# Three vectors of a two-layer graph and state-space kernel reach all partitions by DMA through DRAM instead of by TensorE, with a new table of steps

## Chip, cores and metric

The kernel runs on one core of a Trainium2 chip. The metric is the device time of one execution in microseconds (us).

## What is computed

x has shape (32, 512, 256): 32 elements of 512 tokens with 256 features; adj has shape (32, 512, 512) and holds 0 and 1. All is fp32. Each element passes two layers, each of a graph part and a feed-forward part, with a layer norm ahead of each and a residual sum after it:

```python
x = x + gat(layernorm(x), adj)      # softmax over j of leaky_relu(f1_i + f2_j) where adj, times Wh
x = x + mamba2(layernorm(x))        # projection, convolution over 4 tokens, scan with 8 heads, output
x = x + gru(gat(layernorm(x), adj), layernorm(x))
x = x + moe(layernorm(x))           # shared MLP + 4 experts, the two best by softmax of x @ gW
```

Three pieces matter here.

- **Attention.** The softmax's exponential of a leaky ReLU is written as a maximum of two products, exp(f1)exp(f2) and exp(0.2 f1)exp(0.2 f2), suitably shifted. So a query factor per token i and a key factor per token j are enough. The matrix is made with j on partitions and i along the row, so the query factors, two rows of 512, have to be present on all 128 partitions.
- **Scan.** The tokens of an element are cut into four pieces of 128. Each state that a piece inherits is weighted by exp of the running sum of dA up to each token, per head. These decays are needed as a row of 128 tokens on all 64 partitions of a head's state.
- **Mixture.** The output of expert e for token i is multiplied by a gate g(i, e). Hidden rows of two experts lie on 64 partitions each with tokens along the row, so g has to be present on 64 partitions.

## The kernel before

TensorE (PE in the profile) does the products, VectorE (DVE), ScalarE (ACT) and GpSimd (POOL) what stands between; SyncE (SP) issues the loads and stores. The weights are loaded once, ahead of the loop, by DMAs issued from ACT.

**Buffers.** `quad` tiles (16 buffers of some 4 KB a partition) hold x, xT, xn, L, query and the like; `row` tiles (26 of 2 KB) hold rows of 512; `bank` is one of the eight PSUM banks, each 128 x 512. A tile's buffer is used again once its last reader is done.

**The order is written out by hand.** An element's work is cut into 20 parts (`PARTS`), each a generator that yields after each small step. `PLAN` gives a turn to each step of each part, `PERIOD` is the distance between successive elements in turns, and all steps of all elements are sorted by `b * PERIOD + turn`. The engines' instruction streams have that order, and each engine runs its own in order, waiting where an input or a buffer isn't ready. A turn has no fixed length; a period of turns has one element's worth of steps, from four or five neighbouring elements.

**The steps concerned.**

- `attention` (L271): the largest f2 by a reduction (L276), a transpose that puts it on all partitions (L279), its maximum (L282) and three multiples (L285). Four transposes of f1, broadcast over 128 columns, put f1 on all partitions (L290, bank `ps_f1`). ACT makes the two query factors from this by ReLU (L294) and exp (L297), each 128 x 512, and the key factors from f2 (L300, L302). For each of four j, ACT multiplies by key1 (L309), DVE takes the maximum with the second product (L312) and masks by adj (L315). The result pT is read by PE at L343 in layer 0 and at L675 in layer 1.
- `steps_of_time` (L382): dt, dA and its running sums by TensorE (L428), laid out with piece and head on partitions as `byS` and `byL`. `byHL` (L436) spreads byL over heads; from both, TensorE makes the differences (L445, two groups with four banks each) and ACT their exponentials (L451, L454), the L of the scan. Then 12 products with a matrix of ones at chosen rows (`kind1`, L461) spread the running sums over 64 partitions in three banks, and ACT takes their exponentials into `ecs` rows (L468).
- `scan` (L546) reads ecs at L577 (last column, for the state) and L579 (POOL multiplies it with C); TensorE uses the product at L620.
- `gates` (L757): few gate logits per token by `narrow`, softmax, the two best, new weights g5 with four repeats (L807) and a column of ones (L798), four transposes (L812), copied as `gT` (L815).
- `mixture` (L860): two products of gT with `pair_of` (L868) spread the gates over partitions, four products with `b3` (L873) start the output with the biases; DVE multiplies the experts' hidden rows by the gates (L877); TensorE adds the shared part and the experts (L884, L886) in two banks, DVE adds them to x (L888), and x is stored (L891).

SP's stream per element has ten DMAs: x (L259), two times four of adj (L267), and the output (L891). None of them feeds on what the kernel itself computed except the last.

Of the kernel before, what the change touches and what calls it, by code (L numbers as in the profile page):

```python
# [11 lines left out]
F32 = mybir.dt.float32  # L12
# [6 lines left out]
P = 128  # L19
N = 512  # L20
# [11 lines left out]
def adj_ffn_kernel(ctx: ExitStack, tc: tile.TileContext, i: dict, out: bass.AP):  # L32
# [36 lines left out]
    pair_of = const.tile([HD, P], F32, name="pair_of")  # L69
    for j in range(2):  # L70
        nc.vector.tensor_copy(pair_of[32 * j:32 * j + 32].rearrange("e (s g) -> e s g", s=2),
                              ident[32 * j:32 * j + 32, 34 * j:34 * j + 2].unsqueeze(2).to_broadcast([32, 2, HD]))
# [8 lines left out]
    kind1 = const.tile([P, HD], F32, name="kind1")  # L81
    nc.vector.tensor_copy(kind1, kinds[:, 1:].to_broadcast([P, HD]))
# [115 lines left out]
    for r in (64, 96):  # L198
        nc.scalar.dma_start(b3[r:r + 4, :], i["L1_ffn_eb3"])
        nc.scalar.dma_start(b3[r + 4:r + 5, :], i["L1_ffn_sb3"].unsqueeze(0))  # L200
# [14 lines left out]
    small = ctx.enter_context(tc.tile_pool(name="small", bufs=2))  # L215

# [54 lines left out]
    def attention(f1, f2, adj, kind):  # L271
# [16 lines left out]
        pf = bank("ps_f1")  # L288
        for t in range(T):
            nc.tensor.transpose(pf[:, t * P:(t + 1) * P], f1[:, t:t + 1].to_broadcast([P, P]), ident)  # L290
        yield
        query = quad("query", 2)
        for n, scale in enumerate((-0.8, 0.8)):
            nc.scalar.activation(query[:, n, :], pf, AF.Relu, scale=scale, bias=nfs[:, n + 1:n + 2])  # L294
            yield
        for n in range(2):
            nc.scalar.activation(query[:, n, :], query[:, n, :], AF.Exp, scale=-1.0)  # L297
            yield
# [7 lines left out]
        for j in range(0, T, 2):  # L306
# [7 lines left out]
            for i, p in both:  # L314
                nc.vector.scalar_tensor_tensor(p, adj[i].bitcast(kind), 2.0 ** -120, p, op0=ALU.max, op1=ALU.min)  # L315
                yield
# [13 lines left out]
    def gnn0(e):  # L330
# [6 lines left out]
        pT = yield from attention(f21[:, 1, :], f21[:, 0, :], e.adj, U32)  # L337
# [28 lines left out]
    def narrow(name, w, vT):  # L366
# [8 lines left out]
        few = small.tile([P, P], F32, name="fewT")  # L375
# [6 lines left out]
    def steps_of_time(e):  # L382
# [51 lines left out]
        yield  # L434
        byHL = quad("byHL", HEADS)
# [5 lines left out]
        e.ecss = [None]  # L441
        for h0 in (0, 4):
# [5 lines left out]
            for c in range(0, T, 2):  # L448
# [4 lines left out]
                for L, _ in both:  # L453
                    nc.scalar.activation(L, L, AF.Exp, scale=-1.0)  # L454
                    yield

        banks = [bank("ps_ecs") for c in range(1, T)]
        for q in range(2):
            for c, ps in enumerate(banks, 1):
                for r in range(2):  # L460
                    nc.tensor.matmul(ps[r * HD:(r + 1) * HD, q * 2 * P:(q + 1) * 2 * P], kind1[32 * c:32 * c + 32, :],  # L461
                                     byHL[32 * c:32 * c + 32, heads_of(q, r), :], start=q == 0, stop=True,
                                     skip_group_check=True)
        yield
        for ps in banks:
            ecs = row("ecs")
            e.ecss.append(ecs.rearrange("p (j l) -> p j l", j=NP))
            nc.scalar.activation(ecs, ps, AF.Exp)  # L468
            yield
# [193 lines left out]
    def gnn1(e):  # L663
# [5 lines left out]
        pT = yield from attention(f21[:, 1, :], f21[:, 0, :], e.adj, I32)  # L669
# [87 lines left out]
    def gates(e):  # L757
# [38 lines left out]
        g5 = row("g5").rearrange("p (t r e) -> p t r e", t=T, r=4)  # L796
        nc.gpsimd.memset(g5[:, :, :, 5:], 0.0)
        nc.gpsimd.memset(g5[:, :, :, 4:5], 1.0)  # L798
# [7 lines left out]
        for t in range(T):  # L806
            nc.vector.tensor_mul(g5[:, t, :, :4], lg[:, t, :].unsqueeze(1).to_broadcast([P, 4, 4]),  # L807
                                 red[:, t:t + 1].unsqueeze(2).to_broadcast([P, 4, 4]))
        yield
        ps = bank("ps_gT")  # L810
        for t in range(T):
            nc.tensor.transpose(ps[:, t * P:(t + 1) * P], g5[:, t, :, :].rearrange("p r e -> p (r e)"), ident)  # L812
# [182 lines left out]
```

## Time and profile before

| | |
|---|---|
| time, median of 3 runs | 3431.26 us (3430.89 to 3432.96) |
| the profiled execution's own time | 3430.99 us |
| its span in the profile | 3429.3 us |
| busy PE / DVE / ACT / POOL | 3367.4 / 2814.7 / 1694.0 / 587.8 us |
| mean granted TensorE clock | 0.996 of full |
| DMA | 110.45 MB, mean 32 GB/s |

In the views of the profile, a line has the kernel's line (L290), the engine, the operation and the tiles `out<-in` with buffer numbers left out; "x256" is a number of instructions. A group shows the busy time and the mean of one in ns, then the idle time of the engine just before it and what ended it. An fp32 product shows as two matmul records (x4 for two products); a transpose as one. Some groups of this profile, as count, mean ns of one and busy us:

| line, what | count | mean ns | busy us |
|---|---|---|---|
| L290 PE, f1 onto partitions | 256 | 275 | 38.9 |
| L461 PE, decays onto partitions | 768 | 387 | 35.4 |
| L868 PE, gates onto partitions | 128 | 640 | 36.1 |
| L873 PE, biases | 256 | 400 | 36.2 |
| L812 PE, gates transposed | 128 | 272 | 19.2 |
| L294 / L297 ACT, query factors | 128 / 128 | 684 / 627 | 81.0 / 73.3 |
| L468 ACT, decays | 96 | 597 | 50.4 |
| L312 / L315 DVE, pT | 256 / 256 | 859 / 681 | 212.0 / 166.5 |
| L807 / L888 DVE | 128 / 64 | 166 / 680 | 13.5 / 43.5 |
| L392 ACT, 128 x 32 | 32 | 229 | 7.3 |

Matmuls are pipelined: the printed lengths overlap, and busy time is their union.

### The profile page before, as it was taken

How to read it: one execution, taken by the hardware profiler on the slowest of the kernel's cores; microseconds unless marked ns; L12 is line 12 of the kernel's file. 1: busy time of each engine (PE TensorE's matmuls, PEld its weight loads, DVE VectorE, ACT ScalarE, POOL GpSimd, SP SyncE). 2: the span in 40 equal slices, each digit the busy share in tenths (PEclk: the TensorE clock that was granted, in tenths of full speed). 3: DMA queues.
4: the chain of work that ended last, by engine and by line, in shares of the span. 5: the costliest groups of instructions: out<-in, count | busy, mean ns of one | idle time of the engine just before them, and what ended most of it. 6: DMA issues, size and time to landing. Idle time of an engine off the chain costs nothing.

```text
span 3429.3 us, 49262 instructions
## 1 busy us (share of the span) xinstructions
PE 3367.4 (98%) x17800; PEld 1979.2 (58%) x17800; DVE 2814.7 (82%) x7625; ACT 1694.0 (49%) x3202; POOL 587.8 (17%) x593
## 2 busy tenths in 40 slices
PE   5999999999999999999999999999999999999998
PEld 3555655565555656555655556565556555565654
DVE  6888888888888888888888888888888888888873
ACT  2455455444555454554445554445544455544453
POOL 0112111112111121111121111221111211112210
PEclk8999999999999999999999999999999999999999
DMA  3001011011001010110110110101101100101000
GB/s 127 22 28 38 22 38 28 25 38 38 23 28 34 29 38 22 37 28 25 38 38 22 28 34 29 38 22 38 28 26 38 38 22 28 35 28 38 19 19 13
DMA packets 78392, 110.45 MB, mean 32 GB/s; under 512 B 8122, under 2 KB 44100, under 8 KB 78148
## 3 DMA queue, kind: packets, MB, share of 16 engines
q1 hardware_dynamic: 71216, 101.34, 9.9%
q10 hardware_dynamic: 6932, 5.96, 0.5%
q8 instruction: 141, 2.31, 0.3%
q14 instruction: 103, 0.84, 0.1%
HBM read 90.50 MB, written 16.78 MB: 31 GB/s over the span
## 4 chain that ended last, share of the span: by engine, by line
PE 95%; DVE 2%; issue 1%; ACT 0%; POOL 0%; DMA 0%; SPq 0%; DVEq 0%; POOLq 0%; ACTq 0%
PE ps_conv L476 8%; PE ps_g L675 7%; PE ps_rz L701 6%; PE ps_mo L657 6%; PE ps_e L837 6%; PE ps_z L538 6%; PE ps_h L343 6%; PE ps_rz L704 6%; PE ps_y L612 3%; PE ps_s L828 3%; PE ps_e L886 3%; PE ps_hn L714 3%; PE ps_g L351 3%; PE ps_in L726 3%; PE ps_seg L445 3%; PE ps_xT L252 2%
## 5 line engine op out<-in xcount | busy, mean ns | idle before, releaser
L483 DVE SCALAR_TENSOR_TENSOR acc<-ps_conv,cw,acc 128x511 f32<-128x511 f32 (+2 forms) x480 | 345.3, 736 | 51.0 <-ACT acc L480 46.5
L734 POOL TENSOR_TENSOR oT<-xT,gate 128x512 f32<-128x512 f32 x64 | 121.0, 1912 | 1130.0 <-ACT gate L731 1130.0
L476 PE MATMUL ps_conv<-xT,win 128*128 128x512 f32 x640 | 291.4, 594 | 0.2 <-ACT xT L254 0.2
L224 POOL TENSOR_TENSOR rstd<-rstd,mhalf 128x4 f32<-128x4 f32 x128 | 160.7, 1256 | 737.9 <-DVE dtd L556 380.4
L254 ACT COPY xT<-ps_xT 128x512 f32<-128x512 f32 x192 | 106.1, 587 | 300.5 <-PE ps_xT L252 300.5
L675 PE MATMUL ps_g<-xn,pT 128*128 128x257 f32 x1024 | 246.9, 383 | 0.7 <-DVE pT L315 0.7
L675 PEld LDWEIGHTS ps_g<-xn,pT 128*128 128x128 f32 x1024 | 191.6, 190 | 92.9 <-issue 37.5
L701 PE MATMUL ps_rz<-xT,whh 128*128 128x512 f32 x512 | 244.0, 599 | 1.2
L538 PE MATMUL ps_z<-xT,win 128*128 128x512 f32 x512 | 242.0, 595 | 0.0
L704 PE MATMUL ps_rz<-go,wih 128*128 128x512 f32 x512 | 240.7, 592 | 0.0
L343 PE MATMUL ps_h<-pT,xn 128*128 128x512 f32 x512 | 231.8, 596 | 8.8 <-issue 8.8
L837 PE MATMUL ps_e<-xT,ew 128*128 128x512 f32 x512 | 236.6, 595 | 0.0
L579 POOL TENSOR_TENSOR ecs<-ecs,cc 128x512 f32<-128x512 f32 x96 | 136.1, 1418 | 546.3 <-DVE end L577 538.0
L657 PE MATMUL ps_mo<-wc,xh 128*128 128x256 f32 x1024 | 226.3, 379 | 0.0
L312 DVE SCALAR_TENSOR_TENSOR pT<-query,key,pT 128x512 f32<-128x512 f32 x256 | 212.0, 859 | 9.9 <-ACT pT L309 9.9
L657 PEld LDWEIGHTS ps_mo<-wc,xh 128*128 128x128 f32 x1024 | 192.1, 190 | 24.8
L476 PEld LDWEIGHTS ps_conv<-xT,win 128*128 128x128 f32 x640 | 121.7, 190 | 140.3 <-issue 137.1
L234 DVE BATCH_NORM_STATS2 st<-x 128x6 f32<-128x256 f32 x512 | 196.6, 416 | 3.3
L480 ACT ACTIVATE acc<-ps_conv,cb,cw 128x512 f32<-128x512 f32 x160 | 124.8, 780 | 138.0 <-PE ps_conv L476 137.4
L241 DVE TENSOR_SCALAR xn<-x,mv,rstd 128x256 f32<-128x256 f32 (+1 forms) x512 | 183.3, 410 | 5.4 <-POOL rstd L224 5.4
L325 DVE SCALAR_TENSOR_TENSOR prod<-xn,wrow 128x256 f32<-128x256 f32 x512 | 187.6, 417 | 0.0
L682 ACT ACTIVATE pT<-ps_g,rs 128x256 f32<-128x256 f32 x128 | 60.7, 474 | 236.8 <-DVE rs L679 236.8
(209 smaller groups left out, 7040.3 us busy)
## 6 DMA issues: line engine op xcount, KB each, us to landing
adj<-in_adjT_dram SPq DMA_DIRECT2D x256, 256.0 KB, 2.8
x<-in_x_dram SPq DMA_DIRECT2D x32, 512.0 KB, 3.9
out_dram<-x SPq DMA_DIRECT2D x32, 512.0 KB, 5.3
win<-in_L_ffn_W_in_dram ACTq DMA_DIRECT2D x1, 1160.0 KB
raw<-in_wihT_dram ACTq DMA_DIRECT2D x1, 768.0 KB, 7.4
whh<-in_whhT_dram ACTq DMA_DIRECT2D x1, 768.0 KB, 8.1
ew<-in_L_ffn_eW_dram ACTq DMA_DIRECT2D x5, 128.0 KB, 3.1
woutT<-in_woutT_dram ACTq DMA_DIRECT2D x1, 512.0 KB, 7.5
```

Source lines behind the costliest of these rows:

```text
L234: nc.vector.bn_stats(st[:, t, :], x[:, t, :])
L312: nc.vector.scalar_tensor_tensor(p, query[:, 1, :], key2[:, i:i + 1], p, op0=ALU.mult, op1=ALU.max)
L325: nc.vector.scalar_tensor_tensor(prod, xn[:, t, :D], 1.0, wrow[:, u, :], op0=ALU.mult, op1=ALU.mult, accum_out=f21[:, u, t:t + 1])
L343: nc.tensor.matmul(ps, xn[:, j, k * P:(k + 1) * P], pT[:, j, :], start=j == 0, stop=j == T - 1)
L476: nc.tensor.matmul(ps, win[:, k, 512 + c * P:512 + (c + 1) * P], e.xT[:, k, :], start=k == 0, stop=k == KD - 1)
L483: nc.vector.scalar_tensor_tensor(acc[:, s:], ps[:, :N - s], cw[:, c, 3 - s:4 - s], acc[:, s:], op0=ALU.mult, op1=ALU.add)
L538: nc.tensor.matmul(ps, win[:, k, j * P:(j + 1) * P], uT[:, k, :], start=k == 0, stop=k == KD - 1)
L657: nc.tensor.matmul(ps[:, :D], xh[:, j, t * P:(t + 1) * P], wc[:, j, :], start=j == 0, stop=j == NP - 1)
L675: nc.tensor.matmul(ps[:, :D + 1], pT[:, j, cut], xn[:, j, :], start=j == 0, stop=j == T - 1)
L701: nc.tensor.matmul(ps, whh[:, k, cols], xT[:, k, :], start=k == 0, stop=False)
L704: nc.tensor.matmul(ps, wih[:, k, cols], e.go[:, k, :], start=False, stop=k == KD - 1)
L837: nc.tensor.matmul(ps, ew1[:, k, m, :], vT[:, k, :], start=k == 0, stop=k == KD - 1)
```

## The change

- **Query factors.** The four transposes of f1 go. ACT makes the two factors by tokens, from the 128 x 4 tile f1, as q8 (128 x 2 x 4). A DMA stores q8 into a DRAM tile `line` of two rows of 512, and a second DMA loads `line` onto all 128 partitions as query.
- **Decays.** ACT takes the exponential of byL (128 x 128), a DMA stores it as `rows`, and a new part `decays_of_states` loads the three ecs rows with four DMAs each, every source row going to 64 partitions. The 12 products, their banks and the three exponentials go.
- **Gates.** g5 has no repeats: one product on DVE, one transpose, a copy of 128 x 128. A DMA stores it as `gates`, four DMAs load it as two `pg` rows, onto 64 partitions each. The products with pair_of go. The biases are made by four products in four row groups into four banks, and x is added per 128 tokens (four DVE additions of 256 columns instead of two of 512). b3 holds four copies of the biases, so the preamble has four more small DMAs on ACT.
- **DMAs.** All new ones in the loop are issued by SP, in the table's order: 32 per element.
- **Table.** 21 parts, PERIOD 424, and a new turn for every step of all parts.

```diff
-        pf = bank("ps_f1")
-        for t in range(T):
-            nc.tensor.transpose(pf[:, t * P:(t + 1) * P], f1[:, t:t + 1].to_broadcast([P, P]), ident)
+        q8 = small.tile([P, 2, T], F32, name="q8")
+        for n, scale in enumerate((-0.8, 0.8)):
+            nc.scalar.activation(q8[:, n, :], f1, AF.Relu, scale=scale, bias=nfs[:, n + 1:n + 2])
+        yield
+        nc.scalar.activation(q8, q8, AF.Exp, scale=-1.0)
+        yield
+        line = dram.tile([2, N], F32, name="line")
+        nc.sync.dma_start(line.rearrange("n (t p) -> p n t", p=P), q8)
         yield
         query = quad("query", 2)
-        for n, scale in enumerate((-0.8, 0.8)):
-            nc.scalar.activation(query[:, n, :], pf, AF.Relu, scale=scale, bias=nfs[:, n + 1:n + 2])
-            yield
-        for n in range(2):
-            nc.scalar.activation(query[:, n, :], query[:, n, :], AF.Exp, scale=-1.0)
-            yield
+        nc.sync.dma_start(query, line.partition_broadcast(P))
+        yield
...
+        eE = small.tile([P, P], F32, name="fewT", bufs=4)
+        nc.scalar.activation(eE, byL, AF.Exp)
+        yield
+        e.rows = dram.tile([P, P], F32, name="rows")
+        nc.sync.dma_start(e.rows, eE)
+        yield
...
+    def decays_of_states(e):
+
+        e.ecss = [None]
+        for c in range(1, T):
+            ecs = row("ecs").rearrange("p (j l) -> p j l", j=NP)
+            e.ecss.append(ecs)
+            for q in range(2):
                 for r in range(2):
-                    nc.tensor.matmul(ps[r * HD:(r + 1) * HD, q * 2 * P:(q + 1) * 2 * P], kind1[32 * c:32 * c + 32, :],
-                                     byHL[32 * c:32 * c + 32, heads_of(q, r), :], start=q == 0, stop=True,
-                                     skip_group_check=True)
...
+                    h = heads_of(q, r)
+                    src = e.rows[32 * c + HEADS + h.start:32 * c + HEADS + h.stop:2, :]
+                    nc.sync.dma_start(ecs[r * HD:(r + 1) * HD, 2 * q:2 * q + 2, :], src.partition_broadcast(HD))
             yield
...
+        nc.vector.tensor_mul(g5[:, :, :4], lg, red.unsqueeze(2).to_broadcast(shape))
         yield
         ps = bank("ps_gT")
-        for t in range(T):
-            nc.tensor.transpose(ps[:, t * P:(t + 1) * P], g5[:, t, :, :].rearrange("p r e -> p (r e)"), ident)
-        yield
-        gT = e.gT = row("gT")
-        nc.scalar.copy(gT, ps)
-        yield
+        nc.tensor.transpose(ps[:, :P], g5.rearrange("p t e -> p (t e)"), ident)
+        yield
+        gT = e.gT = small.tile([P, P], F32, name="fewT", bufs=4)
+        nc.scalar.copy(gT, ps[:, :P])
+        yield
+
+        line = dram.tile([P, P], F32, name="gates")
+        nc.sync.dma_start(line, gT)
+        yield
+        e.pgs = []
+        for j in range(2):
+            pg = row("pg")
+            e.pgs.append(pg)
+            for s in range(2):
+                src = line.rearrange("(t e) p -> e t p", t=T)[2 * j + s]
+                nc.sync.dma_start(pg[s * HD:(s + 1) * HD, :].rearrange("g (t p) -> g t p", t=T),
+                                  src.partition_broadcast(HD))
+            yield
...
+        pes = [bank("ps_e3") for t in range(T)]
+        for t, ps in enumerate(pes):
+            own = slice(32 * t, 32 * t + 32)
+            nc.tensor.matmul(ps[:, :D], gT[own, :], b3[own, :], start=True, stop=False)
+        yield
+        for t, ps in enumerate(pes):
+            tok = slice(t * P, (t + 1) * P)
+            nc.tensor.matmul(ps[:, :D], e.h2[:, tok], sw3, start=False, stop=False)
+            for j in range(2):
+                nc.tensor.matmul(ps[:, :D], e.e2[j][:, tok], ew3[:, j, :], start=False, stop=j == 1)
+            yield
+            nc.vector.tensor_add(x[:, t, :], ps[:, :D], x[:, t, :])
             yield
...
-    PERIOD = 420
+    PERIOD = 424
```

In the new table, the turns of the steps that matter, in an element's own count: layer 0's attention stores line at 138 and loads query at 213, ACT first reads it at 215, PE uses pT from 261 on. The exponential of byL is at 643, rows is stored at 644, ecs loaded at 690 to 692, first read (L577) at 727. Layer 1's attention has the transpose of the maximum at 882, q8 at 885 and 886, line at 887, query at 888, the keys at 889, L309 at 927 and 928, pT complete at 940, L675 from 958 on. The gates are stored at 1498 and loaded at 1549 and 1609; the mixture runs from 1634 to 1662, and the output is stored at 1850.

## The prediction

> **What bounds the kernel now.** I first read the page's shares and its chain of waits.
>
> ```profile
> PE 3367.4 (98%) x17800; PEld 1979.2 (58%) x17800; DVE 2814.7 (82%) x7625; ACT 1694.0 (49%) x3202; POOL 587.8 (17%) x593
> PE 95%; DVE 2%; issue 1%; ACT 0%; POOL 0%; DMA 0%; SPq 0%; DVEq 0%; POOLq 0%; ACTq 0%
> ```
>
> TensorE (PE) is 98% busy and is 95% of the chain that ends last; no DMA and no other engine is on it. A busy PE need not be at its peak, so I went on to the windows: stretches between the starts of the output matmuls (L657) of two successive elements, the stretch ahead of the first of these, and that after the last. The columns are length, then PE, PEld, DVE, ACT, POOL, clock, DMA share, GB/s.
>
> ```profile
> 1048.11:1152.74 104.63, 104.46 (x556) 61.51 (x556) 87.63 (x237) 52.88 (x100) 18.37 (x18) 1.00 0.11 31
> 2094.53:2199.16 104.63, 104.46 (x557) 61.52 (x556) 87.62 (x237) 52.88 (x100) 18.37 (x18) 1.00 0.10 31
> 0.00:118.52 118.52, 75.82 (x390) 42.86 (x391) 80.64 (x228) 38.52 (x73) 13.98 (x31) 0.90 0.33 105
> 3340.59:3429.30 88.71, 79.39 (x304) 45.26 (x302) 35.30 (x116) 27.04 (x50) 6.47 (x9) 0.97 0.04 13
> ```
>
> In the middle an element costs 104.63 us of PE. DVE needs 87.6, ACT 52.9, and the DMA engines are 11% used: all three have room. Only the head has long PE gaps. So time is bought by taking columns off PE, provided nothing new makes it wait. What a step takes on PE I read as the distance from its start to the next start in the PE timeline, since the printed durations overlap:
>
> ```profile
> 1720.49 0.60 PE L290 MATMUL ps_f<-ident,f 128*128 128x128 f32 x4
> 1720.92 1.88 PE L704 MATMUL ps_rz<-go,wih 128*128 128x512 f32 x4
> ...
> 1728.89 0.70 PE L868 MATMUL ps_gb<-gT,pair_of 32*128 32x512 f32 x2
> ...
> 1730.07 1.98 PE L701 MATMUL ps_rz<-xT,whh 128*128 128x512 f32 x4
> ...
> 1737.46 2.12 PE L445 MATMUL ps_seg<-byHL,byS 32*128 32x512 f32 x8
> 1739.51 0.70 PE L884 MATMUL ps_e<-sw,h 128*128 128x256 f32 x2
> ...
> 1743.92 1.14 PE L445 MATMUL ps_seg<-byHL,byS 32*128 32x512 f32 x8
> 1744.99 0.66 PE L563 MATMUL ps_xt<-ident,xh 128*128 128x128 f32 x4
> ...
> 1752.90 1.11 PE L461 MATMUL ps_ecs<-byHL,kind 32*64 32x256 f32 x24
> 1753.94 0.66 PE L586 MATMUL ps_st<-xdd,bt 128*64 128x128 f32 x8
> ```
>
> A transpose takes 0.43 / 4 = 0.108 us. A pair of 512-column matmuls (x4) takes 1.72. Two L445 groups of the same shape take 2.05 and 1.07: the first holds about 0.98 us of waiting for banks that the busy figure hides. The x24 of L461 take only 1.04, because six of them run side by side.
>
> **What the Trainium skill says.** "TensorEngine Tiling (Array Packing)", Key Properties: changing the tile shape drains TensorE. The trace agrees: the matmuls of L701 that follow the 32-row ones take 1.82 us (1730.07 to 1731.89) where 1.72 is usual, so 0.1 us a change. "TensorE: Matmul & The Clock Gate", Part 1: after an idle window the array runs at a lower clock; here the head's clock is 0.90. "DMA: Bandwidth & Descriptors", Specifications: below 512 bytes a write is a read-modify-write; no packet of the trace of before stores to DRAM so small, so no run here shows its price.
>
> **The change part by part, per element, on PE.**
> - Query factors: two attentions lose four transposes each (L290): 8 x 0.108 = 0.87 us.
> - Decays: L461 goes: 1.04 us.
> - Gates: four transposes (L812) become one: 3 x 0.108 = 0.33.
> - Bias and gates (L868, L873): 1.18 us, of which 2 x 0.43 is streaming of 512 columns and 0.32 loading and changing shape. What stays is four 256-column products in four row groups, side by side: 2 x 0.216 + 0.32 = 0.75. Saved 0.43 (0.25 if the passes do not overlap, 0.75 if the overhead halves).
>
> Sum: 2.67 us. **The new table** also moves every other step. Along both tables I count 26 changes of tile shape in a period before and 22 after, of which about two are in the prices above: 0.2 us. In the new order the two L445 groups find only one other bank in use, so the 0.98 us there may go. Against that, it may bring waits that I cannot list. I take a further gain of 0.5 for all of this (bounds -1.0 and +1.0). Together 3.2 us an element.
>
> **The other engines.** DVE: four L807 (0.166 each) become one, two L888 (0.68) become four, each priced as L659 (0.475, PSUM, 256 columns): -0.50 + 0.54, nothing. ACT loses 2 x (2 x 0.684 + 2 x 0.627) + 3 x 0.597 = 7.0 us and gains six small activations at 0.23 and one of 0.28: lighter by 5.3. POOL clears less. None is near 101 us. SP issues 32 DMAs an element instead of 10; an issue takes 0.33 to 0.43, so 12 us. Its waits in order matter little: if rows and quads take the longest free of their 26 and 16 buffers, what a DMA overwrites was free some 100 turns before, and the engine results that it waits for come earlier in the same table. Bytes: 1.0 + 0.8 + 0.6 MB more on 3.1; with 101 us that is 55 GB/s, where one load of x alone moves 512 KB in 3.9 us.
>
> ```profile
> adj<-in_adjT_dram SPq DMA_DIRECT2D x256, 256.0 KB, 2.8
> x<-in_x_dram SPq DMA_DIRECT2D x32, 512.0 KB, 3.9
> out_dram<-x SPq DMA_DIRECT2D x32, 512.0 KB, 5.3
> ```
>
> **The new waits**, each DMA store to DRAM, then a load:
> - Decays: E's exponential at turn 643, rows stored at 644, loads from 690, first use (L577) at 727. The table puts 20 us of PE work between. Store 3.5, twelve issues 5, landing 2.8: 11.3 us. Covered.
> - Gates: store at turn 1498, loads at 1549 and 1609, first use at 1634: 32 us of PE work. Covered.
> - First layer's query: store at 138, load at 213, 15.6 us between. Covered, even behind three adjacency loads.
> - Second layer's query: this is the tight one. TensorE's transpose of the maximum is turn 882, store and load 887 and 888, first reader on ACT 927, first PE reader (L675) 958. Between 882 and 958 stand ten pairs of 512 columns and one narrow product: 10 x 1.72 + 0.57 = 17.8 us. DVE has on its own queue between them nine L483 (0.736), two L494 (0.68), one L542 (0.68), four L241 (0.41), six L325 (0.417 and 0.081), 13.3 us by the rows and some 11.5 with their overlap, then eight steps of L312 and L315 (5.3). So DVE is the pace here, and the query may be late by 11.5 less q8's three activations and the first scaling (1.5): **about 10 us for store plus load**. Behind the reader, ACT queues the convolution's and the experts' evictions; behind L312, DVE queues all else, and PE waits at L675. The load is like x's: 0.4 to issue and 3.9. The store is 1,024 packets of 4 bytes, 64 per DMA engine. Between adj's 2.8 and out's 5.3 I take 3.5. Sum 7.8: hidden, with 2 us to spare.
>
> **Head and tail.** There is nothing to hide behind. In the head, ACT issues four more constants (0.25 to 0.55, 1.5 together), then q8 0.7, store 3.5, load 4.3, against 2.6 for the four activations that go: +7.4. In the tail the last element's second query has 12.1 + 5.3 us of chain against 6.9 of PE work left to it; before, 9.2 against 7.4: +6. The gates' chain now stands ahead of two expert products that covered it: +3. Sum +16.
>
> **Sum.** The profiled execution took 3430.99 us, 1.7 outside its span, 0.3 under the median shown. Thirty full periods give 30 x 3.2 = 96; the first and last element 3 together. 3431 - 96 - 3 + 16 = 3348; I say **3349**.
>
> **Rivals.**
> - Partial gain: the bank wait comes back elsewhere at its 1.0 us. Gain 1.67 an element: 3431 - 50 - 3 + 16 = 3394. For it: DVE's sums above meet PE's to a microsecond, so small errors show. Against: the old table shows only 1 us of such waits in 104.6.
> - The store decides, on the other side. Each 4-byte store waits for its own read-modify-write: at the 0.2 us that the Trainium skill's "DMA: Bandwidth & Descriptors", Latency and other measured facts, gives for an HBM access, 64 x 0.2 + 2.8 = 15.6 us, an estimate. With the load 19.9, so 9.9 over the 10 us budget, and 6.7 net loss an element: 3431 + 201 - 3 + 16 + 24 (head and tail, 12 each) = 3669. It decides from a store of 8.9 us (95 ns a packet) upward. Against: 512-byte packets cannot be that slow when 256 KB lands in 2.8 us.
> - No change: the two cancel at that point, 3431.
> - That the change doesn't do what it says I exclude: the transposes and products are gone from the code.
>
> **Chances.** Forecast, 3322 to 3378: 0.58. Partial gain, 3378 to 3424: 0.16. Within 0.2% (what a measurement can tell from no change, 7 us): 0.05. Slower, 3438 to 3669: 0.21, more than the store alone earns, because a whole new table can hold waits that I did not find. Faster 0.74. The range runs from 3322 (bank waits and overhead gone, 4.0 an element) to 3450, leaving 0.16 above and 0.04 below; the likeliest case's own range is 3322 to 3378.
>
> **What would show it.** A period of about 101.4 us between starts of L657; L290, L461 and L868's lines gone; L445 near 1.07 in both groups; line's landing near 3.5 and query's near 4; DVE waiting for ACT at the first product with query (now L312), and PE for DVE at L675, by no more than a microsecond. I am wrong if line lands later than 9 us, if that product waits for the query each period, or if PE's idle time grows in the middle.

## The result and the profile after

The changed kernel takes **3546.88 us** (median of 4 runs, 3543.45 to 3555.04) where the kernel before, run beside it, takes 3432.11 (3430.89 to 3433.15): a ratio of 1.0338, interval 1.0320 to 1.0356. It is slower by 115 us; the forecast was faster by 82. The profiled execution took 3555.04 us, with a span of 3553.3.

First the page of the changed kernel, the same two lines that the prediction opened with.

```profile
PE 3315.8 (93%) x16552; PEld 1938.5 (55%) x16552; DVE 2864.5 (81%) x7590; ACT 1541.1 (43%) x3074; POOL 581.9 (16%) x593
PE 45%; DVE 24%; DMA 18%; ACT 7%; issue 3%; POOL 2%; SPq 1%; ACTq 0%; DVEq 0%; POOLq 0%
```

PE is busy for 52 us less, as meant, but the span is 124 longer. The chain that ends last, 95% PE before, is now 18% DMA: a transfer has come onto it. The windows of the changed kernel, two successive elements from one start of L657 to the next, then the stretch after the last start (columns: length, PE, PEld, DVE, ACT, POOL, clock, DMA share, GB/s):

```profile
1213.20:1320.20 107.00, 102.53 (x518) 59.84 (x517) 88.64 (x238) 47.98 (x96) 18.12 (x18) 0.98 0.19 54
1320.20:1425.30 105.10, 100.72 (x518) 59.16 (x517) 89.25 (x237) 47.99 (x96) 18.15 (x18) 1.00 0.20 55
3445.40:3553.30 107.90, 85.42 (x319) 47.72 (x317) 37.06 (x118) 27.61 (x53) 5.87 (x9) 0.94 0.11 31
```

These two elements take 107.0 and 105.1 us. Over the 27 in the middle (all but the first two and the last two of the 31 distances between starts) the average is 106.55, where it was 104.64; "period" below is this average. PE idles for about 4.4 us in each of the two; before it was 0.2. The first L657 starts at 143.9 us (118.5 before) and the last stretch is 107.9 long (88.7 before). So the 124 us are 25 in front of the first L657, 19 behind the last, and 79 between, where the first and last elements lose more than those in the middle. Who waits in the middle is in the table of waits of the changed kernel (columns: total us, times, longest):

```profile
ACT pT L305 <- DMA query<-line: 186.6, 43, 17.0
PE ps_z L538 <- ACT oT L719: 87.9, 30, 4.1
PEld ps_z L538 <- ACT oT L719: 112.7, 30, 4.9
```

ACT waits for the query 43 times, and 30 times, about once an element, PE waits at L538, a product of the convolution's input that has nothing to do with the query. The timelines of SP's queue, of ACT and of PE in the second of the two elements join the two:

```profile
1338.46 0.38 SPq L290 DMA_DIRECT2D line<-q  x1
1347.40 0.34 SPq L293 DMA_DIRECT2D query<-line  x1
```

```profile
1347.07 0.78 ACT L480 ACTIVATE acc<-ps_conv,cb,cw 128x512 f32<-128x512 f32 x1
1352.16 2.56 ACT L305 ACTIVATE pT<-query,key 128x512 f32<-128x512 f32 x4 [4.32 <-DMA query<-line]
1354.63 0.24 ACT L372 COPY fewT<-ps_dt 128x128 f32<-128x128 f32 x1
1354.77 0.59 ACT L540 ACTIVATE sz<-ps_z 128x512 f32<-128x512 f32 x1
1355.26 1.26 ACT L719 ACTIVATE oT<-ps_hn,bhh 128x512 f32<-128x512 f32 x2
```

```profile
1351.42 1.88 PE L538 MATMUL ps_z<-xT,win 128*128 128x512 f32 x4
1355.99 1.99 PE L538 MATMUL ps_z<-xT,win 128*128 128x512 f32 x4 [2.69 <-ACT oT L719]
1357.82 1.47 PE L675 MATMUL ps_g<-xn,pT 128*128 128x257 f32 x6
```

The store of line is issued at 1338.46. SP can issue the load only when it has landed, at 1347.40: **8.9 us**. The load ends with L305's start, 4.8 us later: 13.7 us where there were 10 to spare. ACT stands 4.32 us at L305, and behind it in its queue stand the evictions L372, L540 and L719, whose PSUM banks the next L538 of PE needs. So PE stops two products ahead of the one that reads pT.

Over the 27 elements the load is issued 9.3 us behind the store on average (8.3 to 10.8), L305 starts 4.6 us behind the load, and ACT stands 4.5 us. For most of the store's time nothing moves. The windows from its issue to two microseconds later, and from there to the load's issue (columns as above):

```profile
1338.46:1340.46 2.00, 2.00 (x6) 0.87 (x5) 1.96 (x3) 1.55 (x5) 0.00 (x0) 1.00 0.23 2
1340.46:1347.40 6.94, 6.94 (x21) 2.84 (x23) 6.87 (x14) 4.47 (x9) 0.00 (x0) 1.00 0.00 0
```

The DMA engines are at work in the first two microseconds alone; in the seven that follow they are idle, and SP still waits for the store.

The stall is not all that PE loses. In the first of the two elements, that of 107.0 us, the four matmuls behind it take 3.68 us where they take 1.99 in the second, and the granted clock of that stretch is 0.52:

```profile
1249.35 3.68 PE L538 MATMUL ps_z<-xT,win 128*128 128x512 f32 x4 [3.03 <-ACT oT L719]
```

```profile
1249.30:1252.72 3.42, 3.37 (x4) 1.43 (x5) 3.42 (x11) 1.06 (x2) 0.00 (x0) 0.52 0.00 0
```

The trace has such stretches at half the clock, 3.4 or 6.8 us in all, in 22 of the 27 elements, and in none of the 27 before the change.

### The profile page after: what moved, and what is told of

It reads as the page before. It is cut to its first block, busy times and chain, and to the rows that moved or that the text cites. A ratio compares the mean times of both kernels' runs of the same rounds, so it can differ in the third digit from the quotient of the medians.

```text
span 3553.3 us, 48385 instructions
## 1 busy us (share of the span) xinstructions
PE 3315.8 (93%) x16552; PEld 1938.5 (55%) x16552; DVE 2864.5 (81%) x7590; ACT 1541.1 (43%) x3074; POOL 581.9 (16%) x593
## 4 chain that ended last, share of the span: by engine, by line
PE 45%; DVE 24%; DMA 18%; ACT 7%; issue 3%; POOL 2%; SPq 1%; ACTq 0%; DVEq 0%; POOLq 0%
DMA line<-q 10%; PE ps_g L675 6%; DMA query<-line 6%; PE ps_h L339 5%; DVE prod L321 4%; PE ps_y L612 3%; PE ps_g L347 3%; PE ps_rz L704 3%; PE ps_z L538 3%; PE ps_e L847 3%; DVE st L229 3%; ACT pT L305 3%; DVE xn L236 2%; PE ps_rz L701 2%; PE ps_xt L563 2%
## 5 line engine op out<-in xcount | busy, mean ns | idle before, releaser
L308 DVE SCALAR_TENSOR_TENSOR pT<-query,key,pT 128x512 f32<-128x512 f32 x256 | 236.5, 964 | 170.9 <-ACT pT L305 170.5
L538 PE MATMUL ps_z<-xT,win 128*128 128x512 f32 x512 | 278.6, 684 | 87.9 <-ACT oT L719 87.9
L476 PE MATMUL ps_conv<-xT,win 128*128 128x512 f32 x640 | 299.0, 598 | 0.5 <-ACT xT L249 0.5
L675 PE MATMUL ps_g<-xn,pT 128*128 128x257 f32 x1024 | 259.8, 397 | 13.0 <-DVE pT L311 12.6
L675 PEld LDWEIGHTS ps_g<-xn,pT 128*128 128x128 f32 x1024 | 204.3, 203 | 98.4 <-issue 50.0
L305 ACT ACTIVATE pT<-query,key 128x512 f32<-128x512 f32 x256 | 167.1, 713 | 187.0 <-DMA query<-line 186.6
L321 DVE SCALAR_TENSOR_TENSOR prod<-xn,wrow 128x256 f32<-128x256 f32 x512 | 248.2, 543 | 0.0
L832 ACT ACTIVATE e<-ps_e,eb 128x512 f32<-128x512 f32 x192 | 129.0, 687 | 251.3 <-PE ps_e L847 250.3
L538 PEld LDWEIGHTS ps_z<-xT,win 128*128 128x128 f32 x512 | 106.0, 213 | 233.8 <-issue 120.9
L657 PE MATMUL ps_mo<-wc,xh 128*128 128x256 f32 x1024 | 229.8, 383 | 0.0
L657 PEld LDWEIGHTS ps_mo<-wc,xh 128*128 128x128 f32 x1024 | 194.9, 193 | 25.6
## 6 DMA issues: line engine op xcount, KB each, us to landing
pg<-gates SPq DMA_DIRECT2D x128, 128.0 KB
```

The costliest lines, as they stand in the source:

```text
L305: nc.scalar.activation(p, query[:, 0, :], AF.Identity, scale=key1[:, i:i + 1])
L321: nc.vector.scalar_tensor_tensor(prod, xn[:, t, :D], 1.0, wrow[:, u, :], op0=ALU.mult, op1=ALU.mult, accum_out=f21[:, u, t:t + 1])
L476: nc.tensor.matmul(ps, win[:, k, 512 + c * P:512 + (c + 1) * P], e.xT[:, k, :], start=k == 0, stop=k == KD - 1)
L538: nc.tensor.matmul(ps, win[:, k, j * P:(j + 1) * P], uT[:, k, :], start=k == 0, stop=k == KD - 1)
L657: nc.tensor.matmul(ps[:, :D], xh[:, j, t * P:(t + 1) * P], wc[:, j, :], start=j == 0, stop=j == NP - 1)
L675: nc.tensor.matmul(ps[:, :D + 1], pT[:, j, cut], xn[:, j, :], start=j == 0, stop=j == T - 1)
```

## The experiments

**Theory 1**: the 4-byte store lands some 6 us later than the 3.5 us of the forecast, so the second layer's query is late in each element. **Rivals**: the added traffic slows the engines (the page counts 253,000 packets, 78,000 before), and the new table's own order costs the time. All ratios are against runs of the kernel before on the same chip. "Kernel 1" is that of experiment 1, and so on.

**1. The store in its own order.** Only the place of each word in line changes, so that a partition's eight words are one packet. The load stays as it is and now brings the factors in another order than L305 and L308 take them to be in; so this kernel does the same work, but its output is not the wanted one:

```
-        nc.sync.dma_start(line.rearrange("n (t p) -> p n t", p=P), q8)
+        nc.sync.dma_start(line.rearrange("n (p m) -> (n p) m", m=2 * T), q8.rearrange("p n t -> p (n t)"))
```

> The changed kernel, with q8 stored as it lies: 128 packets of 32 bytes, not 1,024 of 4. The load reads the same bytes as before, so the query factors come in another order (values only, the work is the same). Theory 1, the scattered store completes too late for the second layer's query: line lands in 2.5 to 4 us instead of 9 to 10, ACT waits for query by under 1 us at L305, the 4.06 us of lost time at L538 in each element go and about 7 us each in head and tail: 3547 - 31 x 4.06 - 14 = 3407 us, period about 102.3. Rival traffic (the added packets slow everything): a third of the added packets are gone, so a third of the loss at most, about 3500. Rival order (the new table's own waits): 3547, period 106.4.

Measured: 3385.03 us, ratio 0.9861 (0.9846 to 0.9876), 22 less than theory 1 had. One line of the change holds 162 us, more than the whole loss. SP's queue, the same two instructions in this kernel, then one element's window:

```profile
1266.40 0.33 SPq L290 DMA_DIRECT2D line<-q  x1
1268.00 0.33 SPq L293 DMA_DIRECT2D query<-line  x1
```

```profile
1235.30:1337.10 101.80, 100.36 (x518) 59.18 (x516) 89.14 (x236) 47.99 (x96) 18.16 (x18) 1.00 0.17 55
```

The load follows the store after 1.6 us, not 8.9; ACT's waits for the query fall from 186.6 us to 13.6, and the period is 101.76 where the prediction had 101.4. Theory 1 holds; GB/s are as in the changed kernel, so it isn't the bytes. The 4.79 us that the period gives back are 2.9 of PE's idle time (4.16 to 1.25 on average) and 1.9 of its busy time (102.39 to 100.51): kernel 1 has no stretch at half the clock in the middle. The expectation had 4.06.

**2. The query on TensorE again, in the new table.** The eight lines from q8 to the load give way to the four transposes and the two Relu and two Exp of 512 columns.

```
+        pf = bank("ps_f1")
+        for t in range(T):
+            nc.tensor.transpose(pf[:, t * P:(t + 1) * P], f1[:, t:t + 1].to_broadcast([P, P]), ident)
...
-        line = dram.tile([2, N], F32, name="line")
-        nc.sync.dma_start(line.rearrange("n (t p) -> p n t", p=P), q8)
...
-        nc.sync.dma_start(query, line.partition_broadcast(P))
```

> The changed kernel with its table, but the query factors made on TensorE again (four transposes, two Relu and two Exp of 512 columns on ACT, at the turns where q8, its store and load stood); decays and gates still go through DRAM. Theory 1: no wait for query; the 4.06 us at L538 go, four transposes twice cost 0.87: 31 x 3.2 = 99 less, head and tail some 10 less each: 3428 us, period about 103.2. Rival order: 3547 + 27 = 3574, period 107.3. Rival traffic: two of five thousand packets an element gone, about 3520.

Measured: 3410.56 us, ratio 0.9936 (0.9921 to 0.9951), period 102.98. Theory 1 had 3428, the order 3574: as the cause of the loss, the order falls. The new table with decays and gates through DRAM, and the query on TensorE, is 1.66 us an element shorter than the kernel before.

**3. The same, with the transfers beside it.** As 2, and q8, its store and its load to a tile that nobody reads:

```
+        nc.sync.dma_start(line.rearrange("n (t p) -> p n t", p=P), q8)
...
+        spare = quad("spare", 2)
+        nc.sync.dma_start(spare, line.partition_broadcast(P))
```

> As the kernel with the query on TensorE, and beside it q8, its store and its load are still issued at their turns, into a tile that nobody reads. Theory 1 (the lateness of the data is the cost, not the transfer): within 10 us of the kernel without that traffic, about 3430; line still lands 9 to 10 us after its issue. Rival traffic: near the changed kernel, 3540 or more.

Measured: 3457.83 us, ratio 1.0074 (1.0059 to 1.0089), 47 more than 2, period 104.22. Neither theory had that. Either the transfers or the three small activations that fill q8 did it, so those came alone.

**4. The small activations without the transfers.** As 3, without its two DMAs.

> The kernel with the query on TensorE in the changed kernel's table, with q8's three small activations on ACT beside it, but no store and no load of it. The one with store and load as well took 47 us more than the one without. If ACT's extra instructions made that, 3455; if the transfers made it, 3412, as without.

Measured: 3449.98 us, ratio 1.0051 (1.0036 to 1.0066). So 39 of the 47 us are ACT's extra instructions. From start to start on PE, the products that read pT take longer, those of the second layer (to ps_g) by 0.55 us an element and those of the first (to ps_h) by 0.32, and those to ps_bc by 0.30. The period is 104.23, that of 3: in the middle the traffic costs nothing. The other 8 us are the head, where the first L657 starts at 134.1 with the transfers and at 126.0 without. The rival of the traffic falls.

**5 and 6. One layer at a time.** The wide store under `if kind is I32` (second layer) or `if kind is U32` (first layer), the 4-byte one otherwise. The layer with the wide store has its factors in the other order again.

> The changed kernel, with q8 stored as it lies (128 packets of 32 bytes) in the second layer alone (query factors in another order there, the work is the same). Theory 1 (only the second layer's budget is broken; the first layer's store lies under other work outside the head): the middle loses its whole wait, period 101.8, and the time is that of the kernel with both stores wide, 3385, plus the first layer's late store in the head, 8 to 10 us: 3394. Rival traffic: half of what both stores gave, about 3466.

Measured: 3397.99 us, ratio 0.9902 (0.9887 to 0.9917), period 101.80. ACT waits 0.8 us an element for the first layer's query, so its 4-byte store only just fits; PE loses nothing by it.

> The changed kernel, with q8 stored as it lies in the first layer alone (query factors in another order there, the work is the same). Theory 1: the period stays at 106.5, the head alone gains 8 to 10 us: 3538. Rival traffic: about 3466.

Measured: 3561.29 us, ratio 1.0379 (1.0364 to 1.0395), period 107.15. The first L657 comes at 127.7 us instead of 143.9, a larger gain than expected, but the period rises by 0.6 us, PE waits longer at L538 again, and nothing is won. There the second layer's store takes 10.0 us on average to the issue of the load, not 9.3, and ACT stands 5.1 us an element for the query, not 4.5; why the same store takes longer stays open. The main point stands: the second layer's store alone sets the middle, the first layer's the head.

**7. The readers behind the evictions.** In the table the second layer's L305, L308 and L311 go from turns 927 to 940 to behind turn 951:

```
-         ... 889, 927, 928, 931, 932, 933, 934, 935, 936, 937, 938, 939, 940, 958,
+         ... 889, 951.1, 951.15, 951.2, 951.25, 951.3, 951.35, 951.4, 951.45, 951.5, 951.55, 951.6, 951.65, 958,
```

> The changed kernel with its 4-byte store, but the second layer's twelve steps from query to pT (L305, L308, L311) are put behind the five evictions of ACT (L372, L540, twice L719) and the L542 that stood after them, up to turn 104, so that no bank that L538 needs waits for query. If the wait at L538 came of ACT's queue alone, TensorE goes on, the 4.1 us go and the time is near 3400. If the data itself is late (theory 1 in its stricter form: pT is ready 5.3 us after query whatever stands ahead), the wait moves to L675 and the time stays at 3547, within 12.

Measured: 3522.45 us, ratio 1.0261 (1.0244 to 1.0278), period 105.5. Its table of waits has another line at the top:

```profile
PE ps_g L675 <- DVE pT L311: 74.4, 63, 12.4
```

In time from start to start on PE, L538 gives back 3.4 us an element and L675 takes 2.1 more. So most of the wait has moved to where the prediction had put it, and the time lies between the two expectations, nearer the second. Of the 4.8 us, about 1 came of the queue of ACT; the larger part is the data itself.

**8. What a store of few bytes costs.** After the last output, the same queue stores to one tile of DRAM, each store behind the one before.

```
+        nc.sync.dma_start(line8, probe)
+        nc.sync.dma_start(line8, probe)
+        nc.sync.dma_start(flat[:2 * N].rearrange("(p m) -> p m", p=P), probe.rearrange("p n t -> p (n t)"))
...
+        nc.sync.dma_start(far[:, 0:1].rearrange("(n t p) o -> p n t o", n=2, t=T), probe.unsqueeze(3))
...
```

> The changed kernel, and after its last output nine stores by the same queue, each into the same DRAM tile, so that each waits for the one ahead: twice 1,024 packets of 4 bytes as q8's, 128 of 32 bytes, 512, 256 and 128 of 4 bytes, 1,024 of 4 bytes each 64 bytes apart, 512 of 8 bytes, 128 of 4 bytes 64 bytes apart. Theory 1a (the number of packets sets it, 64 packets an engine one after the other): about 9, 9, 1.5, 5, 3, 2.4, 9, 5, 2.4 us. Theory 1b (neighbours of 4 bytes in one 64-byte block wait for each other): the two with a distance of 64 bytes land in 2 to 3 us, the dense ones as in 1a. Theory 1c (it was the traffic of other DMAs at that point): the first two land in under 4 us here, where nothing else moves.

The timeline of SP's queue behind the last output, from the second store on (the first starts while the output is still moving); a store's price is the distance to the next line:

```profile
3606.87 0.36 SPq L956 DMA_DIRECT2D far<-probe  x1
3617.61 0.33 SPq L957 DMA_DIRECT2D far<-probe  x1
3619.02 0.36 SPq L958 DMA_DIRECT2D far<-probe  x1
3627.94 0.36 SPq L959 DMA_DIRECT2D far<-probe  x1
3637.50 0.33 SPq L960 DMA_DIRECT2D far<-probe  x1
3646.88 0.36 SPq L961 DMA_DIRECT2D far<-probe  x1
3649.97 0.36 SPq L962 DMA_DIRECT2D far<-probe  x1
3654.29 0.33 SPq L964 DMA_DIRECT2D far<-probe  x1
```

1,024 packets of 4 bytes: 10.7 us (L956). 128 of 32 bytes: 1.4 (L957). 512, 256 and 128 of 4 bytes: 8.9, 9.6, 9.4 (L958 to L960). 1,024 of 4 bytes, 64 bytes apart: **3.1** (L961). 512 of 8 bytes: 4.3 (L962). So the number of packets doesn't set it (1a falls), nor does other traffic, for nothing else moves here (1c falls). What sets it is how close the packets lie: 128 dense words take three times as long as 1,024 scattered ones. 1b is about right for those and wrong about the dense ones, which it took from 1a: 128 take as long as 512. Packets that lie side by side behave as if their writes waited for each other; no trace shows the writes themselves.

**9. How near is a neighbour.** As 8, with stores of one word a partition.

> The changed kernel, and after its last output nine stores of 4 bytes a partition, each into the same DRAM tile, so that each waits for the one ahead: 128 partitions dense (twice), 32 dense, 128 at a distance of 8, 16 and 32 bytes, 16 dense, 4 dense, 1. Theory 1b (writes of one small block, of 64 bytes say, wait for each other at 0.55 us each): 9.4, 9.4, 9, 4.5, 2.5, 1.5, 9, 2.4, 1.4 us: what counts is how many share a block, not how many there are. If the block is 512 bytes: 9.4, 9.4, 3.4, 4.7, 2.8, 1.9, 2.4, 1.6, 1.4 us. If it is a fixed price of such a dense store: 9 us in every dense case, 1.4 in the others.

The same view, L954 to L962 in the order of the expectation:

```profile
3556.07 0.45 SPq L954 DMA_DIRECT2D far<-probe  x1
3564.29 0.32 SPq L955 DMA_DIRECT2D far<-probe  x1
3572.23 0.33 SPq L956 DMA_DIRECT2D far<-probe  x1
3576.84 0.33 SPq L957 DMA_DIRECT2D far<-probe  x1
3581.07 0.32 SPq L958 DMA_DIRECT2D far<-probe  x1
3583.53 0.32 SPq L959 DMA_DIRECT2D far<-probe  x1
3585.98 0.32 SPq L960 DMA_DIRECT2D far<-probe  x1
3587.30 0.30 SPq L961 DMA_DIRECT2D far<-probe  x1
3588.42 0.22 SPq L962 DMA_DIRECT2D far<-probe  x1
```

8.2 and 7.9 us for 128 dense; 4.6 for 32 dense; 4.2, 2.5 and 2.5 for 128 at 8, 16 and 32 bytes; 1.3 for 16 dense and 1.1 for 4. A block of 64 bytes falls (it gives 9 us to 16 dense words), and so does a fixed price. The sizes follow the 512-byte form within 1.5 us, though 32 dense is dearer and 16 dense cheaper than it says. How large the block is, and why 16 dense are so cheap, stays open; so does whether words of one partition, stored one by one, would cost the same.

**10. Rows of 512 bytes.** q8 is turned by one transpose and stored as eight rows; one product of ps_z stands ahead of it (turn 479 to 465.2), and transpose, store and load go to turns 889.3 to 889.5 in the second layer; in the first, store and load go to turns 143 and 143.5.

```
+        pq = bank("ps_q8")
+        nc.tensor.transpose(pq[:2 * T, :P], q8.rearrange("p n t -> p (n t)"), ident)
...
+        nc.scalar.copy(q8T, pq[:2 * T, :P])
...
+        nc.sync.dma_start(line.rearrange("n (t p) -> (n t) p", p=P), q8T)
```

> The changed kernel with q8 turned by one transpose on TensorE (128 x 8 to 8 x 128), copied by ACT and stored as 8 rows of 512 bytes; one product of ps_z is put ahead of that transpose so that TensorE doesn't wait for q8. Theory 1: line lands in about 3 us, 1.3 us later issued; ACT waits for query by under 1.5 us; PE pays 0.22 an element: 3547 - 31 x 3.7 - 10 = 3422 us, period about 102.6. Rivals order and traffic: 3520 to 3550.

Measured: 3390.34 us, ratio 0.9877 (0.9861 to 0.9894), period 101.97; the load is issued 1.4 us behind the store (1268.28 and 1269.65). Theory 1 had 3422. One small transpose where there were four, and the way through DRAM is hidden in the middle: ACT waits for no query there. Unlike kernel 1, this one brings the factors in the order of their readers.

**11. The wide store, read with a stride.** As 1, and L305 and L308 read every eighth word, so that the factors stand in their order without a transpose.

```
+        asked = query.rearrange("q n f -> q (n f)").rearrange("q (p n t) -> q n t p", n=2, t=T)
...
+                nc.scalar.activation(p, asked[:, 0], AF.Identity, scale=key1[:, i:i + 1])
...
```

> The changed kernel with q8 stored as it lies, 128 packets of 32 bytes, loaded as before, and read by L305 and L308 through an access pattern that takes every eighth element, so that the factors stand in the reference's order. If reading with a stride of 32 bytes costs ACT and DVE nothing, 3385 as with the wide store, within 5. If each of the 16 readings an element takes half as long again (0.33 us more), DVE gets 2.6 us longer an element and lies nearer the bound: 3385 to 3440.

Measured: 3458.48 us, ratio 1.0080 (1.0065 to 1.0095), period 104.12. The two readers by line, first in kernel 1, then here (durations in ns: least, median, most):

```profile
L305 ACT ACTIVATE pT<-query,key x256: 704/709/728, 40.2 to 3305.3; 128x512 f32<-128x512 f32 x128
L308 DVE SCALAR_TENSOR_TENSOR pT<-query,key,pT x256: 734/746/1797, 41.0 to 3307.4; 128x512 f32<-128x512 f32 x128
```

```profile
L306 ACT ACTIVATE pT<-query,key x256: 1197/1222/1259, 41.7 to 3381.6; 128x512 f32<-128x512 f32 x128
L309 DVE SCALAR_TENSOR_TENSOR pT<-query,key,pT x256: 1119/1141/2069, 42.9 to 3383.9; 128x512 f32<-128x512 f32 x128
```

A step of 32 bytes costs ACT 72% and DVE 53% more, and the time lies above the dearer expectation, which had half again for each reading. The Trainium skill, "SBUF — State Buffer", Specifications (TRN2), says that full bandwidth needs at least two hits in each line of 16 bytes; a step of 32 bytes has one. The runs agree that it costs, and these are its prices here.

**12 and 13. What the new table lost at ps_xT.** Between the kernel before and kernel 1, one group of PE grew by 1.12 us an element from start to start: the transposes to ps_xT. The timelines of POOL and DVE in the changed kernel:

```profile
1331.53 2.67 POOL L359 TENSOR_TENSOR x<-x,blin 128x1024 f32<-128x1024 f32 x1
```

```profile
1331.58 0.42 DVE L321 SCALAR_TENSOR_TENSOR prod<-xn,wrow 128x256 f32<-128x256 f32 x1
...
1331.92 2.56 DVE L321 SCALAR_TENSOR_TENSOR prod<-xn,wrow 128x256 f32<-128x256 f32 x1
...
1334.42 0.41 DVE L321 SCALAR_TENSOR_TENSOR prod<-xn,wrow 128x256 f32<-128x256 f32 x1
```

The second L321 lasts until POOL's addition is done, 2.1 us longer than its neighbours, and it is on the way to the maximum that PE transposes. The Trainium skill, "SBUF — State Buffer", Who interferes with whom, says that a DVE instruction with two inputs in SBUF contends with a GpSimd instruction that reads SBUF; the trace agrees, with these 2.1 us. Both experiments start from kernel 10. Number 12 puts that addition (turn 505) at turn 666.5, behind POOL's subtraction, and the first layer's adjacency loads at turns 131 to 134, ahead of line's store; 13 has the adjacency loads where they were, and lets the addition wait for a reciprocal of the stage in which DVE has idle time (the edit of 13):

```
+        if late:
+            hold = small.tile([P, 1], F32, name="hold")
+            nc.gpsimd.tensor_copy(hold, late[-1])
         nc.gpsimd.tensor_add(e.x, e.x, blin.unsqueeze(1).to_broadcast([P, T, D]))
...
+            if t == 0:
+                late.append(rs)
...
-        (310, 338, 393, 394, 395, 396, 402, 403, 404, 405, 406, 412, 421, 422, 425, 505),
+        (310, 338, 393, 394, 395, 396, 402, 403, 404, 405, 406, 412, 421, 422, 425, 535.5),
```

> The kernel that stores q8 as 8 rows of 512 bytes, with two edits to the table: the first layer's four adjacency loads stand ahead of line's store (turns 131 to 134; in the head the store held three of them until 32.6 us), and POOL's addition of the bias to x (L363 there) goes behind its L738, so that it no longer holds DVE's L325 on the way to the maximum (one L325 of 2.56 us an element, where 0.41 is usual, and PE waits 1.12 us more at ps_xT than before the change). If that wait goes: 1.0 us an element and 3 us in the head, 3390 - 31 - 3 = 3356. If POOL only holds another step of DVE that PE needs (pT of the first layer, oT), 3387 or more.

Measured: 3439.70 us, ratio 1.0021 (1.0013 to 1.0029), period 103.68. From start to start, ps_xT gives back 1.06 us and ps_h takes 2.7 more. There POOL, with its subtraction (L738) and the addition behind it (L363), holds the first layer's pT on DVE:

```profile
1221.89 3.92 POOL L738 TENSOR_TENSOR oT<-xT,gate 128x512 f32<-128x512 f32 x2 [47.32 <-ACT gate L735]
1225.76 2.82 POOL L363 TENSOR_TENSOR x<-x,blin 128x1024 f32<-128x1024 f32 x1
1222.91 3.44 DVE L312 SCALAR_TENSOR_TENSOR pT<-query,key,pT 128x512 f32<-128x512 f32 x2
1226.28 3.46 DVE L315 SCALAR_TENSOR_TENSOR pT<-adj,pT 128x512 f32<-128x512 uint32 x2
```

Undisturbed, two of either take about 1.4. It came back elsewhere, then, as the second expectation said. The earlier adjacency loads brought nothing: the first output product starts at 128.4 us, 128.0 without.

> The kernel that stores q8 as 8 rows of 512 bytes, with POOL's addition of the bias to x (L363 there) moved to the stage of the second layer's output products (L679), where DVE has idle time: POOL first copies one column of that stage's first reciprocal, and so can't start earlier. If DVE holds no step of PE there: the 1.1 us at ps_xT go and nothing comes back, 3390 - 31 = 3359. If it comes back elsewhere, 3390 or more, as when it went behind L738 (3440).

Measured: **3353.55 us** (3351.40 to 3354.72), ratio 0.9770 (0.9754 to 0.9787), period 100.89. The line of the products in question, as in the changed kernel's L321, and the window of an element:

```profile
L325 DVE SCALAR_TENSOR_TENSOR prod<-xn,wrow x512: 410/418/428, 16.2 to 3265.0; 128x256 f32<-128x256 f32 x171
```

```profile
1208.50:1309.40 100.90, 100.53 (x519) 59.33 (x519) 87.27 (x238) 48.54 (x100) 18.31 (x19) 1.00 0.17 57
```

No L325 takes over 0.43 us; against kernel 10 ps_xT gives back 1.06 us from start to start, and no other group takes more. PE is busy for all but 0.4 us of an element. This version beats both kernels. Its first L657, at 129.5 us, and its last stretch, 101.3 long, are still 11 and 13 us behind the kernel before.

## Why the prediction was wrong, step by step

- **PE's savings: right.** From start to start, between the kernel before and kernel 1: L290 gave 0.87, L461 1.04, L812 0.33, as forecast, bias and gates 0.54 (forecast 0.43). Sum 2.78, forecast 2.67.
- **The new table: mis-sized.** It was to add 0.5 net and added 0.1. L445 gave 1.20 (0.98 was thought possible) and the last products of the experts 0.39, which I had not listed; 1.12 went at ps_xT through POOL's addition, which I had not looked for, and 0.42 at ps_h. The net saving is 2.88 an element (forecast 3.2), so the period without the wait, 101.76, was forecast within 0.4 us.
- **The second layer's query: this step failed.** The load was right within half a microsecond (4.6 on average for 4.3). So was the budget of 10 us: store and load took 13.9 and ACT stood for 4.5, so 9.4 were hidden. The term that failed is the store: "between adj's 2.8 and out's 5.3 I take 3.5"; it took 9.3 on average. Neither row carries it: adj is a load into SBUF, and out stores rows of 1 KB. The prediction itself said that no run showed the price of so small a store, and then used one with 2 us to spare. The reason given against the rival, that 512-byte packets can't be so slow, speaks of another kind of transfer.
- **Where the wait shows: half right.** I had named ACT's evictions as queued behind the reader, and PE waiting at L675. PE waits earlier, at L538, for a bank that one of these evictions frees. Experiment 7 shows that most of the time goes either way.
- **The clock, not in the sum.** A wait was counted at its length. On average it costs PE 2.9 us of idle time an element and 1.9 of longer busy time, because in 22 of 27 elements the matmuls after the stall run at half the clock for 3.4 or 6.8 us. The Trainium skill's "TensorE: Matmul & The Clock Gate", Part 1, says that the clock falls to half after an idle window of about 3.4 us. The trace agrees on the half and differs on the length: stalls of 2.5 to 3.6 us at L538 were followed by it in 22 elements, and stalls of 2.5 to 3.4 us were not in the other five. What decides between them is not shown.
- **The other stores and loads: right.** Decays, gates and the first layer's query lie under other work in the middle: kernel 2 has the first two and gains, kernel 5 has the 4-byte store in the first layer and keeps its period. For the last this is partly luck: the store took more than twice what was assumed, and ACT waits 0.8 us for it.
- **Head and tail: too small.** I had +16, and 3 off for the first and last element. The tail's share, +6, doesn't come out of its own figures: 12.1 + 5.3 - 6.9 less 9.2 - 7.4 is 8.7. Kernel 1, with a store of 1.6 us, has already +33 beside 28 even periods: its span is 47.8 shorter, and 28 x 2.88 = 80.6. Most of what it loses in front is there without any query DMA: kernel 2 starts its first L657 at 124.8 us, 6.3 late, of kernel 1's 10.3. PE's wait for dA in the head is 8 to 10 us in the new kernels where it was 1.4. Whether the table's order or the DMAs of decays and gates do this was not separated. The late stores add 15 in front (143.9 against 128.8) and 8.5 behind (107.9 against 99.4).
- **The rival "the store decides": right in place and sign, not in mechanism.** It had 15.6 us for the store, from one access after the other, and break-even at 8.9 us. The store took 9.3, little more, and the kernel is 115 us slower, not nearly even, because of the clock, the head and the tail. And the price isn't per packet: 64 one after the other on each engine isn't what sets it (experiment 8). The Trainium skill's remark on writes below 512 bytes ("DMA: Bandwidth & Descriptors", Specifications) is no measure by itself: packets of 32 bytes are also below it, and the next DMA is issued 1.4 to 1.6 us behind them.
- What was to show me wrong has shown it: line lands later than 9 us, its reader waits for it in each element, and PE's idle time grew in the middle.

## What to carry to other kernels

A tile that is made by partitions and stored to DRAM word by word, so that neighbours in memory come from different partitions, took some 8 to 11 us to land here where runs of 32 bytes took 1.4, whether it had 128 words or 1,024. Give each partition a run of its own, or turn the tile first so that rows are long; the first was no gain here where the readers then had to take every eighth word (experiment 11), the second was (experiments 10 and 13). Before a step goes through DRAM, price the store from a store of the same form, or bound it so that the forecast holds at the upper end; a transfer with 2 us to spare and an unpriced store can't be counted as hidden. Count a stall of PE for more than its length: here, on average, 2.9 us of idle time came with 1.9 us of slower matmuls. When a data wait appears, look for it on the engine that holds the reader and at what is queued behind: here PE stopped first at the bank that an eviction in that queue should free.

## What the runs showed of the hardware

- Stores of 4-byte packets, one or more from each of 128 partitions: 128 dense ones take 7.9 to 9.4 us, 1,024 that lie 64 bytes apart 3.1. In the element shown, the DMA engines are busy for such a store in the first 2 us alone and idle for the 7 that follow, so the busy share of DMA doesn't show the wait.
- Stalls of PE of 2.5 to 3.6 us were followed by half the granted clock, for 3.4 or 6.8 us, in 22 of 27 elements of the changed kernel.
- Six small activations an element on ACT (1.4 us) cost 1.25 us an element of a kernel whose ACT is busy for half the time (experiment 4): here an engine with room still delayed what stands behind.
- SP needs 0.6 us (the median) to issue each of the twelve loads of decays and the four of gates, where the loads of query take 0.33; the forecast had 0.33 to 0.43 for all.
